# Long convolution and whitening: the last two channel groups image by image, a third Toeplitz buffer, half of a pack on VectorE

## The chip, the cores and the metric

The kernel runs on one core of one Trainium2 chip. The metric is the device time of one execution in microseconds; the median of three runs before the change is 941.27 us (940.22 to 941.31).

A core has TensorE (PE; its weight loads are listed apart as PEld), VectorE (DVE), ScalarE (ACT), GpSimd (POOL) and SyncE (SP), which here only issues DMAs. Sixteen DMA engines move data between main memory and the on-chip memory SBUF. TensorE writes its results to PSUM[...].

## The reference: what is computed

The input is four images of 64 channels, 256 x 256, f32. Layer 0 is a long convolution. For each channel, two filters of 256 taps (one along each axis) come from a small network of sines with a decay; the two-dimensional filter is their outer product, the convolution is causal and as long as the image, and the input times a bias is added:

```python
hx = _implicit_filter(z, Xw1, ..., t, deltas)
hy = _implicit_filter(z, Yw1, ..., t, deltas)
k = jnp.einsum('ijk,imk->ijmk', hx, hy)[0]
...
y = jnp.fft.irfft2(u_f * k_f, s=(fft_size, fft_size))[..., :L, :L]
out = y + x * bias[:, None, None]
```

Layer 1 whitens over channels. It takes every ninth pixel of the four images as samples, forms the 64 x 64 covariance, approximates its inverse square root by five Newton-Schulz steps, and applies that matrix to all pixels less the mean:

```python
x1_s = x1[:, ::STRIDE ** 2]
mean1 = jnp.mean(x1_s, axis=-1, keepdims=True)
xc = x1 - mean1
cov = x1_s @ x1_s.T / x1_s.shape[1] + EPS * jnp.eye(B, dtype=x.dtype)
deconv = _isqrt_newton_schulz(cov, N_ITER)
out = deconv @ xc
```

So no output can be written before the last sample of the last image is in the covariance.

## The kernel before

Line numbers are those of the kernel before.

**Start.** The two filters of all channels are computed on small tiles (L144 to L163) and written to main memory as `g_d`, the first two channels also apart as `g0_d` (L164 to L166).

**Convolution.** The 64 channels go in eight groups of eight (`CG`), and each group over the four images (`NB`): `steps` at L109 lists 32 pairs (g, n), group outermost. A step has an input tile `x` (128 partitions x 8 channels x 2 halves x 256, 16 KB a partition) and an output tile `y` of the same size; each has three buffers in the pool `big`. A group's two filters are matrices with constant diagonals (Toeplitz), read from `g_d` by overlapping rows into a tile `toep` (L171; both filters, eight channels, 16 KB a partition, two buffers). `load_toeplitz` fills one filter and one half of the partitions at a time: four DMAs of 512 KB a group, issued in the four items of the step for image 1 of the group before (L379 to L383).

Within a step the channels go in pairs, four items a step. An item passes through two stages of products: x times the first filter into PSUM, which ACT copies to `o1` (L320); then `o1` times the second filter into PSUM, which DVE evicts with bias times x added into `y` (L325). `group(first, second)` (L302) runs stage one of an item together with stage two of the item two earlier (`pending`), on the two halves of TensorE's rows; the order in which the four column blocks are worked off alternates. After it come up to 2.5 us of waiting DVE pack work, then the store of the two finished channels to `y_d`, one tensor for images 0 and 1 and one for images 2 and 3.

**Packing.** When a step's last pair is stored, nine masked copies on DVE (`pack_ops`, L246 to L249) collect its samples from `y` into `samp[n]`, one 16 KB buffer an image; they are queued in `todo` with an assumed cost and run three to a group. The very last step is packed on TensorE instead: `pack_by_pe` (L225) multiplies four channels of `y` by selection matrices and copies the result from PSUM with one ACT and one DVE copy. `covariance(n)` (L257) is 58 small products over `samp[n]` and a DVE addition.

**The seam.** Covariances of images 0 and 1 stand inside the steps (7, 2) and (7, 3), before their third item (L361). After the loop come: group without a first stage, pack of channels 0 to 3, the last group, the covariance of image 2, pack of channels 4 to 7, the covariance of image 3 (L388 to L394). Then the chain of small matrices (L399 to L488) to the whitening matrix `W` and `shift`.

**Whitening.** 32 pieces of y (128 rows = two images x 64 channels, 4096 pixels, 2 MB) are loaded from `y_d`, multiplied by `W` on TensorE (L506), evicted in place with `shift` by ACT and DVE (L511, L514), and written out by DMAs from POOL (L519). The first and last two pieces go out in quarters, the others whole. The first 13 pieces land in `homes` (L277): buffers of the pools above as they come free, in the order "etisoisoitsos", where e is a pool `epool` of one buffer for this alone, t Toeplitz, i input, s samples, o output. Piece i + 13 reuses the home of piece i once that has been written out (L520). The loads of the first 13 stand in SyncE's order: seven in the last two steps (L384 to L386), six after the last covariance.

**What sets the order.** The convolution is under a manual schedule: on each engine the instructions run in the order of the program text, and each waits for what it needs. SyncE issues x loads (`load_x`, L103), Toeplitz loads, y stores and piece loads in this one order, so an issue that waits holds up those behind it. x is read from (image, channel, row, column) with rows of 1 KB: each item issues two channels of the step after next (L373 to L378). The x of the first two steps stand ahead of everything but one small load (L110 to L113).

Of the kernel before, what the change touches and what calls it, by code (L numbers as in the profile page):

```python
# [45 lines left out]
P, H2 = 128, 2  # L46
# [19 lines left out]
def conv_whiten_kernel(ctx: ExitStack, tc: tile.TileContext, a: dict, out: bass.AP):  # L66
# [5 lines left out]
    epool = ctx.enter_context(tc.tile_pool(name="epool", bufs=1))  # L72
    spool = ctx.enter_context(tc.tile_pool(name="spool", bufs=NB))
    tpool = ctx.enter_context(tc.tile_pool(name="tpool", bufs=2))
    o1pool = ctx.enter_context(tc.tile_pool(name="o1pool", bufs=4))
    dram = ctx.enter_context(tc.tile_pool(name="dram", bufs=1, space=bass.MemoryType.DRAM))
    psA = ctx.enter_context(tc.tile_pool(name="psA", bufs=8, space=bass.MemoryType.PSUM))
# [24 lines left out]

    def load_x(t, g, n, c):  # L103
        nc.sync.dma_start(
            out=t[:, c : c + 2].rearrange("p c b w -> p (c b) w"),
            in_=x[n, g * CG + c : g * CG + c + 2].rearrange("c (b p) w -> p (c b) w", p=P),
        )

    steps = [(g, n) for g in range(C // CG) for n in range(NB)]  # L109
    loaded = {s: new_x(*s) for s in steps[:2]}  # L110
    for step, t in loaded.items():
        for c in range(0, CG, 2):
            load_x(t, *step, c)  # L113

    ident = const.tile([P, P], F32, tag="ident", name="ident")
    make_identity(nc, ident)
# [51 lines left out]
    def new_toeplitz(g):  # L168


        return tpool.tile([P, 2, CG, L], F32, tag="toep", name=f"toep_{g}")  # L171

    def load_toeplitz(t, g, f, half, lo=0, hi=CG):
        source, row = (g0_d, 2 * f) if g == 0 and hi == 2 else (g_d, f * C + g * CG + lo)
        nc.sync.dma_start(
            out=t[half * HP : (half + 1) * HP, f, lo:hi],
            in_=bass.AP(
                tensor=source.tensor,
                offset=source.offset + row * GW,
                ap=[[1, HP], [GW, hi - lo], [1, L]],  # L180
            ),
        )

# [73 lines left out]
    def covariance(n):  # L257
# [17 lines left out]


    homes = [  # L277
        {"t": (tpool, "toep"), "s": (spool, "samp"), "i": (big, "in"), "o": (big, "out"), "e": (epool, "extra")}[k]
        for k in "etisoisoitsos"
    ]  # L280

    def load_y(i):
# [7 lines left out]
    def load_next():  # L290
        loaded[len(loaded)] = load_y(len(loaded))
# [5 lines left out]
    def bank(name):  # L297
        return psA.tile([P, H2, L], F32, tag="psA", name=name)

    orders = [list(range(L // HP)), list(reversed(range(L // HP)))]  # L300

    def group(first, second):  # L302

        units = [[None, None] for _ in range(2)]
        for u in range(2):
            if second is not None:
                g, n, c, _, _, o1s = second
                units[u][1] = (bank(f"p2_{g}_{n}_{c + u}"), o1s[u], toep[g][:, 1, c + u, :])
            if first is not None:
                g, n, c, xt, _, _ = first  # L310
                units[u][0] = (bank(f"p1_{g}_{n}_{c + u}"), xt[:, c + u], toep[g][:, 0, c + u, :])

        toeplitz_products(units, orders[0])
        orders.reverse()
        for u in range(2):
            if first is not None:
                g, n, c, _, _, o1s = first
                o1 = o1pool.tile([P, H2, L], F32, tag="o1", name=f"o1_{g}_{n}_{c + u}")
                for to, fr in ((slice(0, HP), slice(HP, P)), (slice(HP, P), slice(0, HP))):
                    nc.scalar.copy(o1[to], units[u][0][0][fr])  # L320
# [9 lines left out]
        spent = 0.0  # L330
        while todo and spent < 2.5:
            cost, op = todo.pop(0)
            op()
            spent += cost
        if second is not None:
            g, n, c, _, yt, _ = second
            last = (g, n) == steps[-1]
            row = n % 2 * C + g * CG + c
            nc.sync.dma_start(
                out=y_d[n // 2][row : row + 2, :].rearrange(  # L340
                    "c (b p w) -> p (c b) w", p=P, w=L
                ),
                in_=yt[:, c : c + 2].rearrange("p c b w -> p (c b) w"),
            )
            if c == CG - 2 and not last:
                todo.extend(pack_ops(g, n, yt, slice(0, CG)))

    engines = mybir.EngineType
    with tc.manual_schedule(
# [3 lines left out]
        for lo, hi in ((0, 2), (2, CG)):  # L353
            for part in range(4):
                load_toeplitz(toep[0], 0, part // 2, part % 2, lo, hi)
        for i, (g, n) in enumerate(steps):
            xt = loaded_x.pop((g, n))
            yt = big.tile([P, CG, H2, L], F32, tag="out", name=f"y_{g}_{n}")
            for c in range(0, CG, 2):
                item = (g, n, c, xt, yt, [])  # L360
                if g == C // CG - 1 and n > 1 and c == 4:  # L361
                    covariance(n - 2)
                group(item, pending.pop(0) if len(pending) == 2 else None)
                pending.append(item)
                if i == 0 and c == 6:

                    fold = const.tile([P, C], F32, tag="fold", name="fold")
                    nc.vector.tensor_tensor(fold, ident[:, 0:C], ident[:, C:P], ALU.add)
                    twice = const.tile([C, 2, C], F32, tag="twice", name="twice")
                    for u in range(2):  # L370
                        nc.vector.tensor_copy(twice[:, u], ident[0:C, 0:C])

                part = (c - 2) // 2 % 4  # L373
                to = i + 2 if c else i + 1
                if to < len(steps) and to > 1:
                    if part == 0:
# [199 lines left out]
```

## Time and profile before

| | |
|---|---|
| median of the runs | 941.27 us |
| profiled execution, device time | 938.56 us |
| its span, first to last instruction | 936.8 us |
| PE busy / PEld busy | 796.7 / 639.0 us |
| DVE / ACT / POOL busy | 649.5 / 480.7 / 31.7 us |
| DMA | 287.67 MB, 307 GB/s over the span |
| mean granted TensorE clock | 0.956 |

The profile is of one execution. Times inside it count from the first instruction of the span. In a row such as "PE p L205 x320", PE is the engine, p the tile written, L205 the line and 320 the number of records. In listings of groups the columns are: busy time, mean duration in ns, idle time of the engine just before and what ended it. "issue" is time in which an engine waited for nothing that the profile shows. DMA shares are the mean busy share of the sixteen engines and can come out slightly above 1. SPq rows are SyncE issuing DMAs; the time until the data is there is listed as the time to landing.

The convolution's products make up L205, 595.6 us for those with x and 589.3 us for those with `o1` (they overlap). DVE's largest groups are the 279 masked copies of L249 (275.5 us), the whitening evictions of L514 (192.1 us) and the convolution's evictions of L325 (180.6 us).

### The profile page before, as it was taken

The page shows a single profiled execution, that of the slowest core. Times are in us where ns is not written, and L with a number is a line of the kernel's source. Part 1 is how long each engine was busy: PE and PEld are TensorE (multiplying, and loading weights), DVE is VectorE, ACT ScalarE, POOL GpSimd, SP SyncE. Part 2 cuts the span into 40 slices and gives each one's busy share as a digit, 9 for nine tenths or more (in the row PEclk, how much of TensorE's full clock was granted, in tenths as well). Part 3 has the DMA queues.
Part 4 walks back from the last instruction along what each step waited for, and adds up shares of the span by engine and source line. Part 5 has one row for each costly group of instructions (what it writes and reads, how often), then busy time and mean ns, then how long its engine had stood idle before and what let it go on. Part 6 is the DMA issues. An engine that isn't in the chain of part 4 may idle for free.

```text
span 936.8 us, 27864 instructions
## 1 busy us (share of the span) xinstructions
PE 796.7 (85%) x11850; PEld 639.0 (68%) x11850; DVE 649.5 (69%) x861; ACT 480.7 (51%) x792; POOL 31.7 (3%) x71
## 2 busy tenths in 40 slices
PE   2999999999999999999999999999687777766400
PEld 2899999999999999899999999989421111111100
DVE  3058687778768786778687768662399999996600
ACT  2245454544445454445454545330299888876500
POOL 3000000000000000000000000000020000000010
PEclk9999999999999999999999999999799999998755
DMA  7499789779879879879979977899999999999998
GB/s 230 111 250 305 236 243 294 239 232 267 284 231 284 267 229 277 263 234 259 278 231 249 293 233 226 289 395 362 415 362 420 428 431 428 430 429 431 430 431 356
DMA packets 164112, 287.67 MB, mean 307 GB/s; under 512 B 6384, under 2 KB 154261, under 8 KB 156309
## 3 DMA queue, kind: packets, MB, share of 16 engines
q1 hardware_dynamic: 156784, 218.18, 72.3%
q0 software_dynamic: 6336, 67.11, 16.9%
q8 instruction: 94, 1.54, 0.7%
q10 hardware_dynamic: 868, 0.60, 0.2%
q14 instruction: 30, 0.24, 0.1%
HBM read 151.44 MB, written 134.42 MB: 305 GB/s over the span
## 4 chain that ended last, share of the span: by engine, by line
PE 69%; issue 15%; DVE 13%; DMA 1%; ACT 1%; POOL 0%; POOLq 0%; ACTq 0%; DVEq 0%; SPq 0%
PE p L205 65%; DVE yi L514 12%; PE pk L231 2%; PE pc L263 2%; POOL out_dram L519 0%; PE po L506 0%; DMA toep<-g_d 0%; DMA g_d<-scratch 0%; PE ZY L421 0%; DVE scratch L154 0%; PE YT L421 0%; PE pm L147 0%; DVE scratch L151 0%; ACT scratch L150 0%; ACT L439 0%
## 5 line engine op out<-in xcount | busy, mean ns | idle before, releaser
L205 PE MATMUL p<-toep,x 64*64 64x64 f32 (+3 forms) x5120 | 595.6, 287 | 8.0 <-DMA toep<-g_d 6.1
L205 PE MATMUL p<-toep,o 64*64 64x64 f32 (+3 forms) x5120 | 589.3, 285 | 1.3 <-issue 1.2
L205 PEld LDWEIGHTS p<-toep,x 64*128 64x128 f32 (+1 forms) x5120 | 546.3, 168 | 34.0 <-DMA toep<-g_d 6.3
L205 PEld LDWEIGHTS p<-toep,o 64*128 64x128 f32 (+1 forms) x5120 | 542.0, 166 | 13.7 <-issue 2.0
L320 ACT COPY o<-p 64x512 f32<-64x512 f32 x512 | 296.8, 580 | 318.3 <-PE p L205 310.7
L325 DVE SCALAR_TENSOR_TENSOR y<-x,bias,p 128x512 f32<-128x512 f32 x256 | 180.6, 743 | 169.1 <-PE p L205 168.2
L249 DVE COPY_PREDICATED samp<-mask,y 128x448 f32<-128x448 int32 (+1 forms) x279 | 275.5, 988 | 6.4
L514 DVE TENSOR_SCALAR yi<-po,shift 64x512 f32<-64x512 f32 x256 | 192.1, 750 | 22.5 <-PE po L506 15.9
L506 PE MATMUL po<-yi,W 64*64 64x512 f32 x1024 | 150.0, 654 | 62.6 <-DVE yi L514 41.3
L511 ACT ACTIVATE yi<-po,shift 64x512 f32<-64x512 f32 x256 | 174.8, 683 | 41.9 <-PE po L506 34.7
L506 PEld LDWEIGHTS po<-yi,W 64*64 64x64 f32 x1024 | 35.4, 141 | 176.3 <-DVE yi L514 128.7
L519 POOL DMA_DIRECT2D out_dram<-yi x44 | 23.6, 537 | 270.5 <-DMA out_dram<-yi 108.8
L405 POOL MEMSET chain<- 64x64 f32 x1 | 0.1, 144 | 618.6 <-PE p L205 618.6
L263 PEld LDWEIGHTS pc<-samp 128*64 128x64 f32 x464 | 14.3, 137 | 1.7 <-ACT samp L240 0.7
L231 PE MATMUL pk<-y,pick 128*128 128x112 f32 (+1 forms) x72 | 15.3, 386 | 0.0
L263 PE MATMUL pc<-samp 128*64 128x65 f32 x464 | 14.9, 223 | 0.4 <-ACT samp L240 0.4
L231 PEld LDWEIGHTS pk<-y,pick 128*128 128x128 f32 x72 | 14.5, 207 | 0.2
L240 ACT COPY samp<-pk 128x116 f32<-128x116 f32 x2 | 0.5, 270 | 25.8 <-PE pk L231 15.3
L147 PE MATMUL pm<-scratch 128*128 128x128 f32 (+1 forms) x12 | 3.8, 474 | 8.7 <-ACT scratch L156 6.2
L271 DVE SCALAR_TENSOR_TENSOR cov<-pc,cov 128x65 f32<-128x65 f32 x4 | 0.9, 228 | 12.1 <-PE pc L263 12.1
L147 PEld LDWEIGHTS pm<-scratch 128*128 128x128 f32 (+1 forms) x12 | 2.9, 313 | 9.4 <-ACT scratch L156 6.8
L241 DVE COPY samp<-pk 128x116 f32<-128x116 f32 x2 | 0.6, 279 | 11.4 <-ACT samp L240 11.4
(71 smaller groups left out, 46.7 us busy)
## 6 DMA issues: line engine op xcount, KB each, us to landing
x<-in_x_dram SPq DMA_DIRECT2D x128, 512.0 KB, 5.5
y_d<-y SPq DMA_DIRECT2D x128, 512.0 KB, 3.7
yi<-y_d SPq DMA_DIRECT2D x32, 2048.0 KB, 16.5
out_dram<-yi POOLq DMA_DIRECT2D x28, 2048.0 KB, 43.1
toep<-g_d SPq DMA_DIRECT2D x28, 512.0 KB, 10.3
out_dram<-yi POOLq DMA_DIRECT2D x16, 512.0 KB, 10.0
toep<-g_d SPq DMA_DIRECT2D x4, 384.0 KB, 7.6
toep<-g_d SPq DMA_DIRECT2D x4, 128.0 KB, 3.1
```

What stands on the lines that cost most here:

```text
L147: nc.tensor.matmul(pm, lhsT=wt, rhs=hs[u], start=True, stop=True)
L205: mm = nc.tensor.matmul(ps[q : q + w, m, HP * k : L], lhsT=src[parts, k // 2, m * P + q : m * P + q + w], rhs=t[parts, : stop : -1] if k e ...
L231: nc.tensor.matmul(pk[:, b, :, 0:nj], lhsT=pick[:, (s - b) % STEP, :], rhs=yt[:, cs, b, s : s + STEP * (nj - 1) + 1 : STEP], start=(s == 0 ...
L249: nc.vector.copy_predicated(dst, m, src)
L263: nc.tensor.matmul(pc[half], lhsT=samp[n][:, b, j, 0:C], rhs=samp[n][:, b, j, :], start=(b == 0 and j < 2), stop=(b == H2 - 1 and j >= NJ ...
L271: nc.vector.scalar_tensor_tensor(cov, pc, 1.0 / NSAMP, cov, ALU.mult, ALU.add)
L320: nc.scalar.copy(o1[to], units[u][0][0][fr])
L325: nc.vector.scalar_tensor_tensor(yt[:, c + u], xt[:, c + u], bias[:, ch : ch + 1], units[u][1][0], ALU.mult, ALU.add,)
L506: nc.tensor.matmul(po[u][halves[k]], lhsT=W[halves[u]], rhs=yt[halves[u], cols[k]], start=True, stop=True,)
L511: nc.scalar.activation(yt[halves[0], cols[k]], po[0][halves[k]], AF.Identity, bias=shift[halves[k]])
L514: nc.vector.tensor_scalar(yt[halves[1], cols[k]], po[1][halves[k]], shift[halves[k]], None, ALU.add)
L519: nc.gpsimd.dma_start(out=o[:, end - part : end], in_=yt[:, end - part : end])
```

## The change

Six things change together.

- `steps`: groups 0 to 5 as before; then, for each image, groups 6 and 7. The covariances of images 0, 1 and 2 stand before the third item of (7, 1), (7, 2) and (7, 3).
- The Toeplitz pool has three buffers; `epool` is gone. The homes become "tssioitsoitos", again 13, and `early` names the items after which eight of the pieces are loaded, from step 28 on; the other five follow the last covariance in SyncE's order.
- Toeplitz tiles are loaded in eight DMAs a group (filter, half of the partitions, four channels), spread over items by the table `blocks`: over twelve items for groups 1 to 5, over eight consecutive items for groups 6 and 7. Where filter and half differ, the first 64 columns, which no product reads, are left out.
- x is laid out by the host as (image, group, partition, channel, half, column), so that a load of two channels reads 4 KB a partition in one run. The second step's x is loaded after the first Toeplitz loads.
- The last step's channels 0 to 3 are packed by DVE, nine masked copies at half width queued after their last pair is stored; channels 4 to 7 stay with `pack_by_pe`.
- After the loop: both remaining groups one after the other, the rest of the DVE packing, `pack_by_pe`, the covariance of image 3, the remaining piece loads.

```diff
-    tpool = ctx.enter_context(tc.tile_pool(name="tpool", bufs=2))
+    tpool = ctx.enter_context(tc.tile_pool(name="tpool", bufs=3))
...
-            out=t[:, c : c + 2].rearrange("p c b w -> p (c b) w"),
-            in_=x[n, g * CG + c : g * CG + c + 2].rearrange("c (b p) w -> p (c b) w", p=P),
+            out=t[:, c : c + 2],
+            in_=x[n, g][:, c : c + 2],
...
-    steps = [(g, n) for g in range(C // CG) for n in range(NB)]
+    steps = [(g, n) for g in range(C // CG - 2) for n in range(NB)]
+    steps += [(g, n) for n in range(NB) for g in range(C // CG - 2, C // CG)]
     loaded = {s: new_x(*s) for s in steps[:2]}
-    for step, t in loaded.items():
-        for c in range(0, CG, 2):
-            load_x(t, *step, c)
+    for c in range(0, CG, 2):
+        load_x(loaded[steps[0]], *steps[0], c)
...
+        skip = 0 if f == half else HP
         nc.sync.dma_start(
-            out=t[half * HP : (half + 1) * HP, f, lo:hi],
+            out=t[half * HP : (half + 1) * HP, f, lo:hi, skip:],
...
-        for k in "etisoisoitsos"
+        for k in "tssioitsoitos"
...
+    blocks = {}
+    for g in range(1, C // CG):
+        first = 16 * g - 14 if g < C // CG - 1 else 16 * g - 22
+        for part in range(8):
+            k = first + (part * 12 // 8 if g < C // CG - 2 else part)
+            blocks[k // 4, k % 4 * 2] = (g, part)
+
+    early = {(28, 4): 1, (28, 6): 1, (29, 6): 1, (30, 4): 1, (31, 2): 1, (31, 4): 1, (31, 6): 2}
...
+    def pack(time=math.inf):
+        while todo and time > 0:
+            cost, op = todo.pop(0)
+            op()
+            time -= cost
...
-            if c == CG - 2 and not last:
-                todo.extend(pack_ops(g, n, yt, slice(0, CG)))
+            if last and c == CG // 2 - 2 or not last and c == CG - 2:
+                todo.extend(pack_ops(g, n, yt, slice(0, c + 2)))
...
+        for c in range(0, CG, 2):
+            load_x(loaded_x[steps[1]], *steps[1], c)
...
-                if g == C // CG - 1 and n > 1 and c == 4:
-                    covariance(n - 2)
+                if g == C // CG - 1 and n > 0 and c == 4:
+                    covariance(n - 1)
...
-                tg, tn = steps[i if c else i - 1]
-                if tn == 1 and tg + 1 < C // CG and (i or c):
+                if (i, c) in blocks:
+                    tg, part = blocks[i, c]
                     if part == 0:
-                        toep[tg + 1] = new_toeplitz(tg + 1)
-                    load_toeplitz(toep[tg + 1], tg + 1, part // 2, part % 2)
-                if i + 2 >= len(steps) and c > 0:
-                    for _ in range(2 if i + 2 == len(steps) and c == 2 else 1):
-                        load_next()
-
+                        toep[tg] = new_toeplitz(tg)
+                    lo = part % 2 * CG // 2
+                    load_toeplitz(toep[tg], tg, part // 4, part // 2 % 2, lo, lo + CG // 2)
+                for _ in range(early.get((i, c), 0)):
+                    load_next()
         g, n, c, xt, yt, _ = pending[0]
-        group(None, pending[0])
-        pack_by_pe(g, n, yt, slice(0, CG // 2))
-        group(None, pending[1])
-        covariance(NB - 2)
+        for item in pending:
+            group(None, item)
+
+        pack()
         pack_by_pe(g, n, yt, slice(CG // 2, CG))
         covariance(NB - 1)
...
+    x = np.asarray(inputs["x"]).reshape(NB, C // CG, CG, H2, P, L).transpose(0, 1, 4, 2, 3, 5)
+    given = {"x": x, "bias": inputs["L0_conv_bias"], **_laid_out(inputs)}
```

More of the change, by code (lines that the diff above doesn't have):

```diff
@@ L71, in conv_whiten_kernel @@
     big = ctx.enter_context(tc.tile_pool(name="big", bufs=3))
-    epool = ctx.enter_context(tc.tile_pool(name="epool", bufs=1))
     spool = ctx.enter_context(tc.tile_pool(name="spool", bufs=NB))
-    tpool = ctx.enter_context(tc.tile_pool(name="tpool", bufs=2))
+    tpool = ctx.enter_context(tc.tile_pool(name="tpool", bufs=3))
     o1pool = ctx.enter_context(tc.tile_pool(name="o1pool", bufs=4))
@@ L174, in load_toeplitz @@
         source, row = (g0_d, 2 * f) if g == 0 and hi == 2 else (g_d, f * C + g * CG + lo)
+        skip = 0 if f == half else HP
         nc.sync.dma_start(
-            out=t[half * HP : (half + 1) * HP, f, lo:hi],
+            out=t[half * HP : (half + 1) * HP, f, lo:hi, skip:],
             in_=bass.AP(
                 tensor=source.tensor,
-                offset=source.offset + row * GW,
-                ap=[[1, HP], [GW, hi - lo], [1, L]],
+                offset=source.offset + row * GW + skip,
+                ap=[[1, HP], [GW, hi - lo], [1, L - skip]],
             ),
@@ L277, in conv_whiten_kernel @@
     homes = [
-        {"t": (tpool, "toep"), "s": (spool, "samp"), "i": (big, "in"), "o": (big, "out"), "e": (epool, "extra")}[k]
-        for k in "etisoisoitsos"
+        {"t": (tpool, "toep"), "s": (spool, "samp"), "i": (big, "in"), "o": (big, "out")}[k]
+        for k in "tssioitsoitos"
     ]
@@ L328, in group @@
                 )
[L330 to L334, printed above, removed]
+        pack(2.5)
         if second is not None:
@@ L558 @@
     from concourse.bass_utils import run_bass_kernel_spmd
-    given = {"x": inputs["x"], "bias": inputs["L0_conv_bias"], **_laid_out(inputs)}
+    x = np.asarray(inputs["x"]).reshape(NB, C // CG, CG, H2, P, L).transpose(0, 1, 4, 2, 3, 5)
+    given = {"x": x, "bias": inputs["L0_conv_bias"], **_laid_out(inputs)}
     given.update(_constants())
```

## The prediction

> **What bounds the kernel now.** I read the busy shares by slice first. Rows are engines in tenths of 40 slices of 23.4 us; the last row is what the DMA engines moved.
>
> ```profile
> PE   2999999999999999999999999999687777766400
> ...
> DVE  3058687778768786778687768662399999996600
> ...
> DMA  7499789779879879879979977899999999999998
> GB/s 230 111 250 305 236 243 294 239 232 267 284 231 284 267 229 277 263 234 259 278 231 249 293 233 226 289 395 362 415 362 420 428 431 428 430 429 431 430 431 356
> ```
>
> There are two regimes. Up to about 645 us TensorE is full, and until about 600 us the DMA is not; after 645 us the DMA runs at 430 GB/s nearly to the end and TensorE has time to spare. The chain of work in order of time (start, length, what) shows the seam:
>
> ```profile
> 614.94 3.64 PE pc L263 x116
> ...
> 633.22 7.56 PE pk L231 x36
> 640.78 4.37 PE p L205 x38
> 645.15 3.64 PE pc L263 x116
> 648.79 7.57 PE pk L231 x36
> 656.71 3.73 PE pc L263 x116
> 661.58 1.28 ACT L439
> 674.34 3.54 PE po L506 x16
> ```
>
> After the last two convolution groups (the second is the 4.37 us row) everything is serial on TensorE: a half pack, a group, a covariance, the other half pack, a covariance, then 13.9 us of small inverse-root steps to the first whitening product at T0 = 674.3 us. Next, busy time by stretch (columns: PE, PEld, DVE, ACT, POOL, granted clock, DMA share, GB/s):
>
> ```profile
> 560.00:600.00 40.00, 40.00 (x753) 37.55 (x752) 28.39 (x35) 18.55 (x32) 0.00 (x0) 1.00 0.72 224
> ...
> 640.00:646.00 6.00, 6.00 (x74) 5.13 (x75) 1.77 (x3) 0.27 (x1) 0.00 (x0) 1.00 0.76 304
> ...
> 678.60:682.00 3.40, 3.40 (x36) 0.94 (x28) 3.29 (x6) 3.32 (x5) 1.66 (x3) 1.00 0.64 246
> ...
> 850.00:900.00 50.00, 22.18 (x128) 7.31 (x128) 24.19 (x33) 21.84 (x32) 3.73 (x7) 0.72 1.01 430
> ```
>
> Before 600 us the DMA has a quarter free and TensorE never waits. After T0 it must write 67.1 MB and read 19 of 32 pieces (39.8 MB): 106.9 MB / 0.430 = 249 us of the 262.5 us left. So the end is T0 plus a nearly fixed stretch, provided the 13 pieces that have a home are in by then. SyncE's timeline (start, length of the run of issues) says they barely are:
>
> ```profile
> ...
> 634.47 11.85 SPq L339 DMA_DIRECT2D y_d<-y  x2
> 646.38 40.55 SPq L287 DMA_DIRECT2D yi<-y_d  x7
> ```
>
> Six of the seven fill homes 8 to 13; the seventh, at 686.6 us, reuses a home. The sixth left at 660.50 and took about 19.1 us (the landing of the one before it), so piece 13 landed near 679.6, 5.3 us after T0.
>
> [...] 224 GB/s at share 0.72 is 311 GB/s at full share for mostly 1 KB packets, against 430 at 1.01 with the 16 KB rows of the tail. [...] the chain's windows show 0.50 from 664 to 674 us, before and, I assume, after.
>
> **The change, part by part.** Let Tc be the end of the last convolution group, 645.15 now.
>
> Half of the last pack moves to DVE. This removes 36 pack rows, 7.56 us, from TensorE between the last two groups: −7.56. On DVE it adds nine copies on 4 channels. The page has the 8-channel ones by form: 155 of 448 elements at 973 ns, 124 of 464 at 1006, so 2.06 ns an element and about 511 and 528 ns at half width: 4.7 us. They start when DVE has evicted the last group and run under the remaining TensorE pack (7.57 us); 2.9 us of cover are left. With no saving from half width (9 × 0.99 = 8.9 us) the last covariance would start 1.3 us late; that is the upper bound.
>
> The covariance of image 2 moves from behind the last group to the middle of the last step. TensorE still does it (3.64 us): 0. But it covered something. At present DVE's last two evictions run from 644.32 to 645.93, 0.78 us past Tc, and the covariance hides that. Now the remaining pack follows the group directly and needs all four channels. Moreover the two last groups stand back to back, and between their evictions DVE does two evictions (1.41), three pack copies of image 3 (3.0) and a small one (0.18), 4.6 us against 4.37 of TensorE, so it comes 0.2 late; then 1.41 us of evictions: +1.65 us of idle TensorE. TensorE has the pack, the last covariance and the whole chain queued behind this wait. Bounds: 0.8 (DVE on time) to 3 (one more burst of three copies ahead of the evictions). The covariance's own DVE addition (0.23) moves with it. Sum to T0: −7.56 + 1.65 = −5.9, so T0 is 668.4. Tc is 645.15 + 3.64 − 7.56 = 641.2.
>
> Image by image with earlier piece loads. Images 0 and 1 are complete after step 27 of 0 to 31, not 29, so reading starts near 560 us (11 groups of 4.55 us before the one that now ends at 610.2) instead of 597.2. Eight pieces, not seven, are issued inside the loop; five, not six, remain. The last two of the eight go out near 633.4 us (loop end 629.1 + 3.64, plus an eviction). From there 7 pieces and two y stores, 15.7 MB, take 36.6 us at 430 GB/s: 670, plus about 2 of latency. Piece 13 lands at 672 against 679.6: −7.6. The end follows T0 (−5.9) and piece 13 (−7.6), and lies between; I take −6.7. What the early reads cost: behind piece loads, x channels for step 30 issued after the first group of step 29 are needed six groups and a covariance later, 31 us, and the longest x landing after the start is 12.6 us: 0, hidden by TensorE. Each early piece waits on SyncE for its home, with y stores and x loads queued behind it; each home was freed at least a group earlier (the sample buffer of image 2 by the covariance just before), so 0.
>
> Third Toeplitz buffer: needed since groups 6 and 7 are live together; it takes the space of the removed extra buffer, so homes stay 13. Each Toeplitz load waits for a buffer freed at least a step before: 0.
>
> Toeplitz in eighths, without columns that no product reads: 64 issues instead of 36, at 0.66 us (5.30 us for eight) 18 us more of SyncE, which waits 397 us for evictions anyway; bytes down an eighth. x in 4 KB rows: less DMA time where the DMA has a quarter free. Both 0 while TensorE sets the pace; had that cover gone, they would be gains. At the start, the second x tile moves behind the first Toeplitz loads: its four issues (1.3 us each, 10.33 for eight) leave the queue ahead of a store that waits for the filter to 16.45 anyway; the Toeplitz loads left at 18.84, when the DMA was at share 0.22. So −0.2, from 0 to −0.8.
>
> Sum: −6.7 − 0.2 = −6.9, a span of 929.9. The profiled execution took 938.56 with 1.76 us around its span, and the median of the runs is 941.27, 2.7 above it; the same step from the median gives **934.4 us**.
>
> **Rivals.** (a) DMA bytes alone set the end: the stretch from 600 us is full, so only the one piece moved out of it counts, 2.1 MB or 4.9 us; 936.4. For: shares of 1.0. Against: 0.51 to 0.76 around 645 us and 246 GB/s after T0, so T0 does bind. (b) The tail gains more: with reads done before the first writes, the slow start (246 to 334 GB/s until 690 us, some 4 us below 430) shrinks, and the four pauses in instruction issue inside the convolution (0.6 to 1.1 us each) go with the lighter DMA: 929. Against: the start is also limited by DVE, 0.5 MB per two 0.75 us evictions. (c) It doesn't do what it says: DVE's copies run at full price and come late, and pieces queue until the evictions as now: −7.56 + 3 + 1.3 = −3.3 at T0, piece 13 no better, halfway −1.6: 939.6. (d) Slower: x behind early pieces. If an x load in steps 28 to 31 lands as late as the 2 MB writes of the saturated tail (43.1 us in the median), 12 us past its 31, TensorE stops for these 12 in step 30 and again in part in step 31 (say 16): 941.3 − 6.9 + 16 = 950. It decides from 40 us of landing on. Against it: step 28 carries 8.4 MB in 18.2 us, about 1.3 us more than 430 GB/s, and step 29 one piece less.
>
> **How the numbers follow.** My forecast 0.55 (931.5 to 937), (a) 0.15, (b) 0.12, (c) 0.07, (d) and unnamed stalls 0.11. A measurement tells about 0.2% from no change, 1.9 us: below 939.4 lie the forecast, (a) and (b), 0.82; within, 0.09; slower, 0.09. The range 929.3 to 941 holds the forecast, (a), (c) and half of (b), some 0.83; the upper end takes in a DVE pack at full price and a lost tail gain.
>
> **What would show it.** One pack of 36 rows instead of two before T0; 1.0 to 2.0 us of TensorE idle before it, ended by DVE's eviction; nine 0.5 us copies ended before that pack; T0 at 667 to 669.5; eight piece loads before the last group, the first near 560; no TensorE wait for x, Toeplitz or pieces before Tc; 261 to 263 us from T0 to the end. It would be wrong if TensorE idles inside steps 24 to 31, if copies at half width cost as much as at full, or if the time after T0 grows by what T0 gains.

## The result, and the profile after

The changed kernel takes 928.51 us (median; 927.77 to 930.36) beside 941.29 (940.22 to 943.36) for the kernel before on the same chip: 0.9865 of it, 95% interval 0.9842 to 0.9887. It is faster, as forecast, but by 12.8 us instead of 6.9, and so 0.8 us below the range. Its profiled execution took 930.36 us, with a span of 928.2; it is the slowest of the four.

The busy shares by slice of the kernel after (40 slices of 23.2 us, tenths):

```profile
PE   3999999999999999999999999999787777765400
...
DVE  3058687768777877787677866667599999996500
...
DMA  4698888888888888879997769989999999999998
GB/s 145 189 275 257 251 258 261 248 258 258 252 251 262 260 248 261 262 237 280 284 277 236 234 189 332 326 288 392 417 407 429 430 428 429 431 430 431 431 430 340
```

The DMA row is smooth where that of before swung between 7 and 9 with every group's Toeplitz loads, and TensorE is full up to the seam as before. The chain of work of the kernel after, at the seam (start, length, what):

```profile
615.47 3.64 PE pc L266 x116
...
635.79 0.84 issue
636.63 1.43 DVE y L343 x2
638.19 7.71 PE pk L234 x36
646.29 3.73 PE pc L266 x116
651.16 1.28 ACT L454
...
663.92 3.69 PE po L521 x16
```

There is one pack by TensorE instead of two, the covariance of image 2 has gone into the step, and TensorE waits for DVE's evictions ahead of the pack, 1.3 us by the list of groups. (The "issue" piece at 635.79 is not TensorE's: the chain runs through DVE there, which is busy with pack copies until 636.6.) T0, the first whitening product, is at 663.9 us instead of 674.3; the granted clock ahead of it was 0.50 in both (655 to 664 us here, 664 to 674 us before). DVE's and SyncE's timelines of the kernel after, at the same place:

```profile
636.63 1.42 DVE L343 SCALAR_TENSOR_TENSOR y<-x,bias,p 128x512 f32<-128x512 f32 x2
637.94 5.88 DVE L252 COPY_PREDICATED samp<-mask,y 128x232 f32<-128x232 int32 x9
```

```profile
629.89 0.95 SPq L290 DMA_DIRECT2D yi<-y_d  x2
633.86 4.58 SPq L353 DMA_DIRECT2D y_d<-y  x2
638.49 41.80 SPq L290 DMA_DIRECT2D yi<-y_d  x6
```

The nine half-width copies take 5.88 us and end 2.1 us before TensorE's pack does. The last two early pieces leave at 629.9, and the last piece that has a home leaves at 650.1 and lands 25.3 us later, at 675.4: that is 11.5 us after T0, where piece 13 landed some 5.3 us after it before. Busy time by stretch of the kernel after:

```profile
560.00:600.00 40.00, 39.59 (x712) 36.85 (x706) 28.27 (x35) 18.52 (x32) 0.00 (x0) 1.00 0.92 328
...
640.00:646.00 6.00, 5.89 (x29) 5.51 (x27) 3.65 (x6) 0.03 (x1) 0.00 (x0) 0.72 0.99 415
678.60:682.00 3.40, 3.04 (x20) 0.94 (x24) 3.31 (x5) 3.30 (x6) 0.54 (x1) 1.00 1.08 398
850.00:900.00 50.00, 16.55 (x96) 5.56 (x96) 18.01 (x24) 16.40 (x24) 4.27 (x8) 0.69 1.01 431
```

At 640 us the DMA is full (0.99 for 0.76) and after T0 too (398 GB/s for 246), so the tail is now one full transfer from before T0 on.

To see where 12.8 us went I profiled the kernel before once more: 941.4 us of span, near its median, while the profile that the prediction rests on was one of its quicker executions (936.8). Against this second profile the span is 13.2 us shorter:

| part | second profile of before | after | difference |
|---|---|---|---|
| pauses of TensorE in "issue" between the first product and the seam | 6.65 | 0.86 | −5.8 |
| first product of the convolution | 22.0 | 20.7 | −1.3 |
| the seam (a pack less, an eviction wait more) | | | −6.4 |
| not placed, inside the convolution | | | −1.1 |
| T0 | 678.5 | 663.9 | −14.6 |
| T0 to the end | 262.9 | 264.3 | +1.4 |

Against the first profile, the one that the prediction used, the same parts are −2.3, −1.4, −6.6 and −0.1, so T0 is 10.4 us earlier; +1.8 after T0 leaves 8.6 us of span, where 6.9 was forecast. The seam is close to the forecast. The pauses are not in the forecast's sum at all, and most of the experiments are about them.

### The profile page after: what moved, and what is told of

Same layout as the page of the kernel before. It is cut to its first block, busy times and chain, and to the rows that moved or that the text cites. A ratio compares the mean times of both kernels' runs of the same rounds, so it can differ in the third digit from the quotient of the medians.

```text
span 928.2 us, 27807 instructions
## 1 busy us (share of the span) xinstructions
PE 788.6 (85%) x11814; PEld 631.0 (68%) x11814; DVE 653.6 (70%) x869; ACT 480.9 (52%) x791; POOL 31.8 (3%) x71
## 4 chain that ended last, share of the span: by engine, by line
PE 69%; issue 15%; DVE 9%; ACT 3%; DMA 2%; POOL 0%; POOLq 0%; ACTq 0%; DVEq 0%; SPq 0%
PE p L208 65%; DVE yi L529 8%; ACT yi L526 3%; DMA yi<-y_d 2%; PE pc L266 2%; PE pk L234 1%; POOL out_dram L534 0%; PE po L521 0%; DMA toep<-g_d 0%; DVE y L343 0%; PE ZY L436 0%; PE YT L436 0%; DVE scratch L154 0%; DVE samp L252 0%; PE pm L147 0%
## 5 line engine op out<-in xcount | busy, mean ns | idle before, releaser
L252 DVE COPY_PREDICATED samp<-mask,y 128x448 f32<-128x448 int32 (+3 forms) x288 | 281.0, 976 | 6.6
L234 PE MATMUL pk<-y,pick 128*128 128x112 f32 (+1 forms) x36 | 7.7, 390 | 1.3 <-DVE y L343 1.3
L234 PEld LDWEIGHTS pk<-y,pick 128*128 128x128 f32 x36 | 7.3, 259 | 1.7 <-issue 1.7
L131 POOL TENSOR_SCALAR pick<-ident,rows 128x128 f32<-128x128 f32 x9 | 5.7, 649 | 0.0
```

The lines of the kernel that those rows point to most:

```text
L131: nc.gpsimd.tensor_scalar(pick[:, s, :], ident, rows[:, s : s + 1], None, ALU.mult)
L234: nc.tensor.matmul(pk[:, b, :, 0:nj], lhsT=pick[:, (s - b) % STEP, :], rhs=yt[:, cs, b, s : s + STEP * (nj - 1) + 1 : STEP], start=(s == 0 ...
L252: nc.vector.copy_predicated(dst, m, src)
```

## The experiments

Times are medians with their range; ratios are against the kernel before, run on the same chips (medians there 941.7 to 943.3). "Pauses" is the sum of TensorE's "issue" pieces in the chain between the first product and the seam.

**The kernel before, unchanged (b_again).**

> The kernel before, unchanged: a second profile of it. Theory P (pauses): the span missed by more than T0 and the tail because TensorE's short pauses in instruction issue (3.0 us in the first profile of before, 0.6 in that of the changed kernel) vary with the DMA load; this profile shows 2 to 6 us of them before 645 us, and a run that is 2 to 3 us longer than the first profile has them longer by about that. Rival V (variation elsewhere): pauses stay at 3.0 and the difference to the first profile lies after T0.

942.93 us (937.42 to 945.14), ratio 1.000 (0.9986 to 1.0015), eight pauses, 6.65 us. In the chain of this run the largest two are

```profile
80.83 1.38 issue
...
380.85 1.39 issue
```

The quicker profile of before had 3.1 us of them. The 14 runs here spread over 7.7 us and 18 in a later job over 13, the four of after over 2.6. The pauses come at 73 to 81, 236, 309, 381, 454, 520 and 626 us: up to 520 mostly 66 to 73 us apart, which is about four steps, the period of the Toeplitz loads.

**The layout of x alone, and its removal from the changed kernel (b_xrows, a_oldx).**

```diff
-            out=t[:, c : c + 2].rearrange("p c b w -> p (c b) w"),
-            in_=x[n, g * CG + c : g * CG + c + 2].rearrange("c (b p) w -> p (c b) w", p=P),
+            out=t[:, c : c + 2],
+            in_=x[n, g][:, c : c + 2],
```

> Before, with x laid out by the host in 4 KB rows and nothing else. Theory P: less DMA time in the convolution, pauses in issue fall from 3.0 us to under 1, the first product starts about 1 us earlier (21 instead of 22.1), T0 about 3.5 earlier, time 3 to 4 us lower. Rival H (hidden, as the prediction costed it): pauses stay near 3, time within 1 us of before.

> The changed kernel with x in its old layout (1 KB rows). Theory P: pauses of 2 to 4 us come back, T0 at 666 to 668, time 3 to 4 us above the changed kernel. Rival H: within 1 us of the changed kernel.

b_xrows: 945.3 us (940.27 to 949.61), 1.0025 (1.001 to 1.004), 8.2 us of pauses. a_oldx: 929.01 us (927.41 to 929.12), 0.9853 (0.9832 to 0.9873), 0.2 us of pauses. Longer rows are worth nothing in either kernel: neither does x in 1 KB rows make the pauses, nor do 4 KB rows take them away.

**Half of the last pack on DVE alone (b_halfpack).** The kernel before with `pack_ops` for channels 0 to 3 of the last step, and both last groups back to back; the covariance of image 2 stays behind them.

```diff
-            if c == CG - 2 and not last:
-                todo.extend(pack_ops(g, n, yt, slice(0, CG)))
+            if last and c == CG // 2 - 2 or not last and c == CG - 2:
+                todo.extend(pack_ops(g, n, yt, slice(0, c + 2)))
...
-        pack_by_pe(g, n, yt, slice(0, CG // 2))
         group(None, pending[1])
         covariance(NB - 2)
+        pack()
```

> Before, with the last step's channels 0 to 3 packed on DVE and the two last groups back to back; the covariance of image 2 stays behind the last group, where it covers DVE's evictions. Theory T (T0 sets the end): T0 7.6 us earlier, end 7 to 7.6 earlier. Rival B (bytes set the end): the six late pieces start when the DMA has finished the two before, about 640 instead of 646, so piece 13 lands about 6 earlier and the end moves 4 to 6.

934.86 us (931.95 to 939.31), 0.9920 (0.9894 to 0.9946). T0 668.4 against 678.5, T0 to the end 264.2. With a covariance to cover the evictions the seam is 7.4 us shorter (7.6 against the first profile), nearly the whole removed pack. Pauses (5.0 us) remain; they are 1.7 us fewer than in b_again, about what is given back after T0 (1.3).

**The spreading of the Toeplitz loads, alone and taken back (b_toep, a_burst).** b_toep is the kernel before with two buffers and the eighths over twelve items; a_burst is the changed kernel with the whole 512 KB loads in four consecutive items.

```diff
-        first = 16 * g - 14 if g < C // CG - 1 else 16 * g - 22
-        for part in range(8):
-            k = first + (part * 12 // 8 if g < C // CG - 2 else part)
+        first = 16 * g - 11 if g < C // CG - 1 else 16 * g - 22
+        for part in range(4):
+            k = first + part
```

> Before, with the Toeplitz loads alone as in the change: eighths without the unread columns, spread over twelve items (for every group; two buffers are enough for that). Theory Z (bursts): TensorE's pauses in issue come one to two steps after each burst of four 512 KB Toeplitz loads (73.6, 80.8, 236, 309, 381, 454, 520 us in the second profile of before) and go when the loads are spread: pauses before 645 us under 1.5 us instead of 3 to 8, runs within 3 us of each other instead of 8, median 936 to 939 against 942.7. Rival O (order or third buffer): pauses depend on something else in the change, here unchanged: 942.7 within 1.5.

> The changed kernel with the Toeplitz loads of before: four of 512 KB in four consecutive items, unread columns included. Theory Z: 3 to 8 us of pauses come back, median 932 to 936 against 928.5. Rival O: 928.5 within 1.5.

b_toep: 934.03 us (932.38 to 934.46), 0.9897 (0.9877 to 0.9918), 0.6 us of pauses, T0 668.9. a_burst: 942.5 us (935.28 to 948.25), 0.9988 (0.9965 to 1.0012), 10.1 us of pauses, T0 677.3. So this part, which the prediction priced at 0, is worth 9 us in the kernel before. Taken out of the changed kernel it costs about as much as the other parts gain: in their new order the whole loads make more pauses (10.1 us) than in the old (6.65). The chain of a_burst where it is worst:

```profile
374.92 3.87 PE p L207 x100
378.79 3.42 issue
382.21 2.91 PE p L207 x18
```

**Size, number or place of these loads (b_apart, b_eburst).** b_apart: before's whole 512 KB loads, but three items apart. b_eburst: the eighths without the unread columns, two an item, in before's four items. The first two lines are of b_apart, the last two of b_eburst.

```diff
+        for part in range(4):
+            k = 16 * g - 14 + 3 * part
...
+        for part in range(8):
+            k = 16 * g - 11 + part // 2
```

> Before, with its four 512 KB Toeplitz loads a group whole, unread columns included, but three items apart instead of in consecutive items. Theory Z1 (it is the bunching that fills the DMA for some 28 us and so starves TensorE's instruction supply): pauses under 2 us, median 934 to 937. Rival Z2 (it is the size of one load, or its unread bytes): pauses of 3 to 8 us remain, median 940 to 943.

> Before, with eighths and without the unread columns, but two in each of four consecutive items, where the kernel before has its bursts. Theory Z1: an eighth fewer bytes in the burst, so pauses of 2 to 6 us, median 938 to 942. Rival Z2: pauses under 1 us, median 933 to 936 as with the spread eighths.

b_apart: 934.65 us (933.61 to 936.3), 0.9908 (0.9882 to 0.9935), 0.75 us of pauses. b_eburst: 937.84 us (935.55 to 940.87), 0.9944 (0.9925 to 0.9963), 2.2 us. The place in time does most of it: whole loads apart are as good as eighths apart (934.65 and 934.03 us), while an eighth fewer bytes in twice as many loads at the old place leave 2.2 us of pauses and bring about half of the gain.

**Are full DMA engines enough? (a_dummy)** The changed kernel with 48 more copies of 512 KB, two in each of before's four items, from x to main memory; nothing reads them.

```diff
+                        nc.sync.dma_start(out=extra_d[spot], in_=x[n, g][:, c : c + 2])
```

> The changed kernel (Toeplitz loads small and spread) with additional copies of x inside main memory, two of 512 KB in each of four consecutive items of every fourth step (24 MB in all), that no engine waits for. They only fill the DMA. Theory Z1: DMA share near 1.1 for 20 to 30 us after them, pauses of 3 to 10 us, all before 480 us, median 932 to 939 against 928.5. Rival Z3 (pauses come from Toeplitz loads themselves, their source rows 4 bytes apart or their 64 partitions): pauses stay under 1.5 us, median within 1.5 us of 928.5.

929.37 us (928.2 to 930.79), 0.9851 (0.9822 to 0.988), 0.8 us of pauses, with the DMA at a share of 1.03 to 1.08 from 64 to 96 us. Two of these stretches, with the columns as before:

```profile
76.00:80.00 4.00, 4.00 (x104) 3.81 (x103) 0.70 (x2) 1.15 (x3) 0.00 (x0) 1.00 1.04 395
...
88.00:92.00 4.00, 4.00 (x103) 3.87 (x98) 3.61 (x5) 2.32 (x4) 0.00 (x0) 1.00 1.07 376
```

One pause of 0.5 us, at 72.3, falls into these 32 us. A full DMA alone is not enough to stop TensorE for long, and my theory of it fell.

**What about a Toeplitz load does it? (d_src, d_rows, d_dst, d_wide)** All four are b_toep with 28 more copies of 512 KB in rows of 1 KB, one in each of before's four items a group; nothing reads them. They differ in one thing at a time:

```diff
+                if 0 < i < 28 and i % 4 == (1 if c else 2):
+                    spot = i // 4 * 4 + c // 2
+                    nc.sync.dma_start(
+                        out=extra_d[spot][:, :, 0:L],
+                        in_=x[n, g * CG : (g + 1) * CG, 0:HP, :].rearrange("c p w -> p c w"),
+                    )
```

This is d_rows: aligned rows of x, into main memory. d_src has the Toeplitz pattern of `g_d` as its source, `ap=[[1, HP], [GW, CG], [1, L]]`. d_dst has an idle on-chip tile as its destination, `extra[spot % 2 * HP : spot % 2 * HP + HP, spot // 2 % 2]`, 64 partitions; d_wide has `extra[:, spot // 2 % 2, spot % 2 * 4 : spot % 2 * 4 + 4]`, all 128.

> The kernel before with its Toeplitz loads in eighths and spread (934.03 us, 0.6 us of pauses of TensorE in instruction issue before the last group), and one additional copy of 512 KB per item in the four consecutive items where the kernel before had its Toeplitz loads: 28 copies, 14.7 MB, read from g_d with the Toeplitz pattern (source rows of 1 KB that begin 4 bytes apart), written to main memory; nothing reads them. Z4 (reading rows that begin 4 bytes apart, bunched, makes the pauses): 3 to 10 us of pauses, 937 to 943 us. Z5 (the destination, 64 partitions of the on-chip memory) and Z7 (neither, but both together, or the wait of the Toeplitz buffers): under 1.5 us of pauses, 932.5 to 935.5 us. Z6 (the bulk of 1 KB packets alone): 3 us or more of pauses, here and in d_rows and d_dst.

> The same as d_src with the same number of copies and bytes, but read from x in rows of 1 KB that begin at multiples of 1 KB, and written to main memory: the control. Z4, Z5 and Z7: under 1.5 us of pauses, 932.5 to 935.5 us. Z6 (the bulk of 1 KB packets alone): 3 us or more of pauses, 937 us or more.

> The same as d_rows, but written to 64 partitions of an on-chip tile that nothing reads. Z5 (bunched writes to 64 partitions make the pauses): 3 to 10 us of pauses, 937 to 943 us, and d_src and d_rows none. Z4 and Z7: under 1.5 us, 932.5 to 935.5 us. Z6: 3 us or more.

> As d_dst (28 additional copies of 512 KB of x in rows of 1 KB, in the items where the kernel before had its Toeplitz loads, nothing reads them), but each copy is written to all 128 partitions of the on-chip tile instead of 64. Z5a (the 64 partitions make it: half as many places take the same bytes): under 1.5 us of pauses, 933 to 936 us, and a landing near the 7.4 us of d_rows. Z5b (any bunched writing to the on-chip memory beside the kernel's own does it): 8 us or more of pauses, 945 to 953 us, as d_dst (12.3 us, 949.28 us).

| | us | range | ratio and interval | pauses | copy to landing |
|---|---|---|---|---|---|
| d_src | 934.44 | 932.05 to 936.34 | 0.9918 (0.9888 to 0.9947) | 0.9 | 7.3 |
| d_rows | 934.32 | 933.72 to 935.6 | 0.9924 (0.9895 to 0.9952) | 1.1 | 7.4 |
| d_dst | 949.28 | 945.07 to 953.64 | 1.0074 (1.0041 to 1.0107) | 13.2 | 10.5 |
| d_wide | 934.51 | 933.27 to 936.08 | 0.9923 (0.9893 to 0.9952) | 1.1 | 8.2 |

(The pauses of d_dst run to its seam at 646 us; the 12.3 us in the expectation of d_wide end at 640.) Of the four only the copies to 64 partitions do it: the same bytes, in rows of the same length, at the same places, to 128 partitions or to main memory cost nothing (934.03 us without any). Busy time by stretch of 4 us (columns as before), first d_rows, then d_dst, then d_wide:

```profile
72.00:76.00 4.00, 4.00 (x44) 3.67 (x42) 3.34 (x5) 2.37 (x5) 0.00 (x0) 1.00 1.06 355
76.00:80.00 4.00, 4.00 (x108) 3.79 (x106) 0.92 (x2) 1.16 (x3) 0.00 (x0) 1.00 1.08 378
```

```profile
72.00:76.00 4.00, 2.42 (x29) 2.02 (x27) 2.73 (x3) 0.94 (x2) 0.00 (x0) 1.00 1.11 321
76.00:80.00 4.00, 4.00 (x44) 4.00 (x42) 1.49 (x2) 2.32 (x4) 0.00 (x0) 1.00 1.13 206
```

```profile
72.00:76.00 4.00, 4.00 (x44) 3.67 (x42) 3.35 (x5) 2.37 (x5) 0.00 (x0) 1.00 1.08 374
76.00:80.00 4.00, 4.00 (x108) 3.79 (x106) 0.91 (x2) 1.16 (x3) 0.00 (x0) 1.00 1.09 333
```

The DMA engines are about as busy in all three; in d_dst they move 206 GB/s in the second stretch instead of 333 and 378 (254 from 64 to 84 us instead of 341 and 349), and TensorE (second number) has 2.42 us of the first 4. Why 64 partitions take the bytes more slowly is in no trace here. Of the 18.5 us between the T0 of d_dst (687.5) and that of d_rows (669.0), the pauses are 12.1, a lower granted clock after a pause 1.7 by estimate (0.5 for 3.4 us from 84.4, a mean of 0.57 from 84 to 88 us) and the start 0.6; some 4 us I have not placed.

**Why TensorE stops.** The list of DMA queues shows a queue of the kind "instruction". In a_burst, over the whole span, and then in the microsecond of 379 to 380 inside the pause of 3.42 us (packets, MB, share):

```profile
q8 instruction: 94, 1.54, 0.7%
```

```profile
DMA packets 252, 0.30 MB, mean 299 GB/s; under 512 B 8, under 2 KB 240, under 8 KB 251
...
q1 hardware_dynamic: 251, 0.28, 105.7%
q8 instruction: 1, 0.02, 6.2%
```

The profile lists the program's instructions among the packets of the sixteen DMA engines. Queue q8 has 94 packets of 16 KB in the kernel before as well, for 24,127 recorded TensorE instructions (matmuls, weight loads and some 430 others), so one packet is worth some 257 instructions (an estimate from these counts), and the packets follow each other by 7.4 us in the median up to 600 us.

The pauses fit a size of 256. TensorE has started 1,473, 1,729, 7,105, 9,665 and 12,225 instructions at the first five pauses of b_again: the steps between them are 1, 21, 10 and 10 times 256. All 43 pauses above 0.3 us before 600 us, in the eleven runs that have any (b_wide apart), stand at the same place of a block of 256. All of them also end 1.2 to 1.7 us after the end of such a packet, though packets start 3 to 12 us apart; and in the longest one the packet itself began after TensorE had stopped (379.71, stop at 378.79). By these places and times TensorE has used up a block of instructions and goes on when the next one is in.

The packets are not slow (0.9 to 1.5 us in most cases), they come late: after TensorE has begun a block the next packet starts 1.4 us later in the median of b_toep and 3.8 at most, but up to 6.8 us later in b_again, 7.0 in a_burst and 6.4 in d_dst. What such a packet waits for is not in the profile. That it waits behind data packets that go to 64 partitions is my guess, from 13.2 us of pauses in d_dst beside 1.1 in d_wide and d_rows.

**The Toeplitz loads themselves on 128 partitions (b_wide).** Same items and bytes, but four loads of one channel to all partitions each.

```diff
+            out=t[:, f, c],
...
+                ap=[[0, 2], [1, HP], [1, L]],
```

> The kernel before with its Toeplitz loads in the same four consecutive items and with the same bytes an item, but each item's 512 KB as four loads of one channel to all 128 partitions, not one load of eight channels to 64 partitions. Z5a: under 1.5 us of pauses of TensorE in instruction issue before the last group, 933.5 to 936 us. Z5b: as the kernel before, 3 to 8 us of pauses, 940 to 945 us.

1066.46 us (1065.56 to 1070.36), 1.1331 (1.1298 to 1.1364): much slower, outside both expectations. It is inconclusive for the question: SyncE needs 6.7 to 10.2 us to issue four of these, longer than an item, so x loads behind them come late (51.6 us of waits of TensorE for x; another 48.3 us in "issue", which I did not follow up). The long "issue" pieces of this run do not stand at one place of a block of 256 instructions, so they are of another kind. Whether the Toeplitz loads themselves would do no harm on 128 partitions stays open.

**When the early pieces are read (a_late, a_early).** The changed kernel with seven pieces in the last two steps as before, or with the last four a little sooner (the table of homes follows). The first added line is of a_late, the second of a_early.

```diff
-    early = {(28, 4): 1, (28, 6): 1, (29, 6): 1, (30, 4): 1, (31, 2): 1, (31, 4): 1, (31, 6): 2}
+    early = {(30, 2): 2, (30, 4): 1, (30, 6): 1, (31, 2): 1, (31, 4): 1, (31, 6): 1}
+    early = {(28, 4): 1, (28, 6): 1, (29, 6): 1, (30, 4): 1, (31, 2): 2, (31, 4): 2}
```

> The changed kernel with seven pieces in the last two steps as before, none earlier, and six after the last covariance. Theory B (bytes after the loop set the end): one piece more in the full stretch, 2.1 MB, and less room before it: 3 to 6 us above the changed kernel, T0 unchanged. Rival T (T0 sets the end): within 1 us of the changed kernel.

> The changed kernel with the last four early pieces one item sooner (two after the second item of the last step, two after the third), homes in the order that this allows. Theory B: the DMA, at a share of 0.74 to 0.87 in 12 of the 20 us before 632 us, is filled there, and the time falls by 1 to 3 us, T0 unchanged. Rival T: within 1 us.

a_late: 931.61 us (930.7 to 935.67), 0.9881 (0.9858 to 0.9903); T0 is 661.4, earlier than after's, but T0 to the end takes 268.4: the last piece with a home lands some 19 us after T0. a_early: 927.96 us (927.45 to 929.39), 0.9839 (0.9819 to 0.9859), T0 662.8 and 262.8 to the end. Reading early is worth about 3 us of the change. The later the last piece with a home lands after T0, the longer the rest takes: 9.8 us and 262.8 in a_early, 11.5 and 264.3 in after, 18.6 and 268.4 in a_late.

**A better one (a_best).** a_early with the covariance of image 2 behind the last group again, where it hides DVE's evictions, at the price of one early piece (`early` ends with (31, 2): 2 and (31, 4): 1).

```diff
-                if g == C // CG - 1 and n > 0 and c == 4:
+                if g == C // CG - 1 and 0 < n < NB - 1 and c == 4:
...
         for item in pending:
             group(None, item)
+        covariance(NB - 2)
```

> The changed kernel with pieces one item sooner as in the run before, and the covariance of image 2 kept behind the last group, where it covers DVE's evictions; that covariance then frees its sample buffer only there, so seven pieces go early and six after. Theory T (T0 sets the end): T0 1.3 us earlier and the end with it, 926.5 to 927. Theory B (bytes set the end): T0 1.3 earlier, the end 0 to 3 us later than with eight early pieces (928 to 931).

926.19 us (925.14 to 927.12), 0.9817 (0.9789 to 0.9846). T0 is 660.2. The chain shows the covariance and the pack closed up:

```profile
625.66 5.54 PE p L208 x58
631.20 3.64 PE pc L266 x116
634.85 7.57 PE pk L234 x36
```

That is 2.3 us below the median of the changed kernel, and their ranges do not meet.

## Why the prediction was right and wrong

**Where it failed.** The step was "Toeplitz in eighths", with the sentence "Both 0 while TensorE sets the pace". TensorE sets the pace only while its instructions arrive, and the profile lists them among the DMA packets (94 of 16 KB in the kernel before; TensorE stood for up to 3.42 us in a_burst until one was in). Spreading the loads took 5.8 us of pauses out (b_again against after), and is worth 9 us alone (b_toep) and 12 to 14 taken back (a_burst; 12 by the ratios, 14 by the medians of two jobs). (The loads in eighths took SyncE 0.94 us each in the median, not 0.66; that did no harm.) The pauses were before me in the chain of waits: rival (b), at 929 us, named all four and tied them to a lighter DMA, though half of its gain was a tail that did not get shorter; that its number came so near to 928.5 is luck. It also blamed the load of the DMA, where a_dummy shows that load alone does not do it. I gave it 0.12, and the profile that I had was one of few pauses (3.1 us, where 6.65 is nearer to the usual), so even a full account from it would have missed about half of their size.

**From span to median.** The sum, −6.9, made a span of 929.9, and 928.2 was measured. That this is only 1.7 us off is partly luck: 4.3 us more came off before T0 than the sum holds (T0 10.4 us earlier in place of 6.1), and the time after T0 grew by 1.8 us where the sum has it 0.8 shorter. Then I took the same 6.9 from the median, 2.7 us above that execution. But the two profiles of before differ by 4.6 us of span, and 3.5 of these are pauses, which the change removes: the kernel after has hardly any. The step "the same step from the median" assumed that what lay between the profile and the median stays. After the change the median lies 1.9 us below the profiled execution.

**The seam: right.** T0 was to gain 5.9 by −7.56 + 1.65. The seam gained 6.4 to 6.6; the wait for DVE was 1.3 us, inside its bounds of 0.8 to 3. One pack, nine copies ended before that pack, as said; the half-width copies took 5.88 us for nine where I had scaled to 4.7, so 2.06 ns an element doesn't hold at half width: a copy of 224 elements took 616 ns beside 973 for 448, from which I estimate a fixed part of 0.26 us. But 7.7 us of cover held. That T0 came to 663.9 and not 668.4 is mostly the pauses and the start.

**Early pieces: half right.** The first left at 563.5, near the 560 of the text, eight went out before the last group, and the last two at 629.9. But "piece 13 lands at 672" became 675.4: the last piece took 25.3 us instead of some 20. (Beside the "about 2 of latency" stands a copy of 2 KB in the kernel before, which landed in 2.0 us.) The sum let seven pieces and two stores run at 430 GB/s from 633.4 us on; in the trace an older y store was still under way then (it landed at 636.7), the DMA moved 350 GB/s from 632 to 636, and the first output writes, from 668.1 on, shared it with the last pieces. The record does not say which of these costs how much. From T0 to the end 264.3 us went by, not 261 to 263: 1.4 to 1.8 us more than before, where the step "between; I take −6.7" has 0.8 us less, and the tail gain of rival (b) did not come. So not all of what T0 gained reached the end.

**x and the third buffer: right.** 0 or no gain for x is what b_xrows and a_oldx show (it even cost 0.25% alone, with 1.6 us more of pauses than b_again). The "less DMA time" came to little: from 100 to 500 us a share of 0.86 at 259 GB/s, x and Toeplitz loads changed together, beside 0.88 at 256 before. No wait of TensorE for x, Toeplitz tiles or pieces stands in its chain between the first product and the last group; rival (d), x behind early pieces, did not happen.

**The start: too small.** −0.2, "from 0 to −0.8", was −1.3. The store of the first filters landed in 1.2 us for 2.4. But kernels with the order of the start unchanged (b_toep, b_apart and b_xrows, first product at 20.7 to 20.8) have the gain too, and d_dst, with the start of b_toep, has hardly any of it (21.8). So the later loading of the second step's x is not shown to be its cause. It stays open.

## What to carry to other kernels

A short "issue" pause of an engine that executes thousands of instructions (24,127 on TensorE here) deserves a look at the DMA queue of the kind "instruction". Here its 94 packets of 16 KB went through the same DMA engines as the data (0.7% of their time in a_burst), and where they came late TensorE stood for up to 3.42 us, while in its chain it waited for no tile. The sign of it was that the pauses stood at multiples of 256 instructions from each other. Spreading the loads that write 64 partitions was worth 9 us (b_toep). Copies of the same bytes to all partitions did no harm at a full DMA (d_wide: 1.1 us of pauses at shares of 1.08 and 1.09), but for the Toeplitz loads themselves that way is not shown to pay: in the one form tried it cost 13% (b_wide). And where runs of one kernel spread by several microseconds, find what differs between two of their profiles before the prediction is made from one of them.

## What the runs showed of the hardware that I had not expected

- With bunched writes to 64 partitions of the on-chip memory TensorE stood in instruction issue for 13.2 us (d_dst), with the same bytes to 128 for 1.1 (d_wide), at a DMA share (1.11 and 1.13 from 72 to 80 us) close to what was harmless with other destinations (1.03 to 1.09 in a_dummy, d_rows and d_wide).
- Instructions take part in the DMA traffic: 94 packets of 16 KB, 1.54 MB, 0.7% of the engines' time in a_burst. By the places of the pauses a packet holds 256 of TensorE's. Where one came late, TensorE stood for up to 3.42 us.
- Rows of 4 KB instead of 1 KB for x gave no time at all (929.01 with 1 KB rows, 928.51 with 4 KB), and source rows that begin 4 bytes apart cost nothing either (d_src, 934.44 us with the copies, 934.03 without any).
- A load that repeats its source rows over two halves of the partitions, one channel of 128 KB, took SyncE 2.6 us to issue in the median (b_wide), against 1.0 for the eighths (b_toep).
